# Layer 1's second chunk: transposed and compressed in the last chunk of layer 0 instead of during the first chunk of layer 1

## The chip, the cores and the metric

The kernel runs on one core of a Trainium2 chip. The metric is the device time of one execution in microseconds; the time before is the median of three runs, 926.27 us (924.6 to 926.37). The engines named below are TensorE (PE in the profile; its weight loads are PEld), VectorE (DVE), ScalarE (ACT), GpSimd (POOL) and SyncE (SP), which here only issues transfers.

## The reference, cut to what matters

Two layers work on `x` of 16 sequences, 256 tokens and 256 channels, in float32. Each computes `x = x + s * g` from the layer norm `xn` of `x`. Layer 0 has a diagonal complex recurrence for `s` and a gated two-matrix network with GELU for `g`. Layer 1, cut to its two halves:

```python
kv = x @ Wkv_a
c_kv, k_rope = kv[..., :64], kv[..., 64:]
k_rope = apply_rope(k_rope)
c_kv = c_kv * rsqrt(mean(c_kv * c_kv) + RMS_EPS) * kv_norm_w      # the compressed keys
# q, k_nope and v for 16 heads; k_rope is shared by all heads
attn = softmax(where(mask, q @ k.T * scale, min))                 # causal, within a sequence
s = (attn @ v) @ Wo

probs = softmax(x @ router_w.T + router_b)                        # 8 experts
top_vals, top_idx = top_k(probs, 2)                               # renormalised to sum 1
g = silu(x @ base_w.T + base_b + SCALING * sum_e gate_e * (x @ lora_A[e]) @ lora_B[e])
```

## The kernel before

Tokens are worked on in 8 chunks of 512 (two sequences), `X[ch]` resident in SBUF as four tiles of 128 tokens. All of layer 0 comes first, chunk after chunk, then all of layer 1. The order of every engine is written out by hand: `InOrder` (line 47) chains each instruction of an engine behind the one issued before it, so the program order of the calls is the order on each queue. Since all instructions pass through that helper, the profile gives almost all of them line 53; they are told apart by their tiles.

**Layer 1's stages for a chunk.** `norm_begin` (235) takes the statistics, `norm_end` (248) writes the normalised rows `xn`. `transpose_chunk` (257) turns them with eight TensorE transposes (`tp`), copied to `xnT` by ScalarE. `kv_begin` (266) multiplies `xnT` by `wkva` (16 matmuls into the PSUM tile `pkv`); ScalarE squares the compressed part, VectorE forms the rotated key parts (four products, into thirds of the tile `tmp`) and the mean square `ss`, GpSimd raises it to the power -0.5 (`rk`) and adds the rotated parts into `row`. `kv_end` (293) scales the compressed part into `row`. `key_chunk` (299) turns `row` into `kT`. `router_chunk` (307) makes the router's logits `lg` and the low-rank products `mid`, then on VectorE the gates of the two chosen experts (one Exp on ScalarE among some twenty small instructions), and multiplies `mid` by them. `mid` of one chunk and `tmp` of the next share one buffer.

**Queries** are made per group of four heads, four tiles a group (`query_mm`, 378): tiles 0 and 1 are the rotary halves, multiplied by cosine and sine on VectorE (`query_mul`, 395), combined on GpSimd (`query_rot`, tile `qrot`) and spread into `qg` by eight transfers on SyncE (`query_move`, 419); tiles 2 and 3 are the latent parts, scaled into `qg` by ScalarE (`query_lat`, 405).

**Layer 1's main loop** runs over 64 units, eight to a chunk: unit `i` is one head group for one of the chunk's two sequences. A unit computes scores in three packs (`score_pack`, 1354: matmuls `sc`, VectorE mask and maximum, ScalarE Exp with its sum into `pr`), normalises them on GpSimd (`normalise`, 1386), turns them in 32 x 32 blocks on VectorE (`turn`, 1399, tile `turned`), and stores them to DRAM with four transfers (`send`, 1411, `far`). The next unit but one fetches them back (`fetch`, 1423, `pT`), and `values` (1442) multiplies them by `row`. SyncE's queue in chunk 0 of layer 1 is thus: `qg` of group 0, of group 1, `far` of unit 0, `pT` of unit 0, `qg` of group 2, `far` of unit 1, `pT`, `far` of unit 2, `pT`, `far` of unit 3, `qg` of group 3, and so on. A fetch waits for its store to have landed, and what stands behind it on the queue waits too.

**Where chunk `ch + 1` is prepared.** In the loop: `norm_end(ch + 1)` in unit 2 for later chunks, `transpose_chunk` at the end of unit 2, `kv_begin` at the end of unit 4, `kv_end` in unit 5, `router_chunk` at the end of unit 6, `key_chunk` in unit 7.

**The passage between the layers** is the last chunk of layer 0 (from line 1222). Layer 1's chunk 0 is normalised, turned, compressed and routed there, and the query tiles of group 0 and most of group 1 are made, between the last matmuls of layer 0 (`mix`, tile `pf`; `outs`, tile `py`) and the last additions (`finish0`, 791, tiles `dx` and `x`: two of chunk 7's halves on GpSimd, chunk 6's four instructions on VectorE). Of chunk 1, only `norm_begin(1)` and `norm_end(1)` are there. PSUM tiles of this passage come from a ring of four banks (`ps_mm`, 452), used in turn by every call of `m1` (224); layer 1 then has a pool of five banks for them and one of three for scores (1285), on the same memory. `dtmp`, `stb` and `cst` are tiles of layer 0's pool `w0`, used last by chunk 6's sums (`zf_early`, 967).

Of the kernel before, what the change touches and what calls it, by code (L numbers as in the profile page):

```python
# [11 lines left out]
F32 = mybir.dt.float32  # L12
I32 = mybir.dt.int32
AF = mybir.ActivationFunctionType
ALU = mybir.AluOpType
AX = mybir.AxisListType
PSUM = bass.MemoryType.PSUM

P = 128
# [4 lines left out]
TPC = CH // P  # L24
# [5 lines left out]
NOPE, ROPE, VD, KVL = 128, 64, 128, 64  # L30
# [11 lines left out]
def tile_two_layers(ctx: ExitStack, tc: tile.TileContext, d: dict, out: bass.AP):  # L42
# [162 lines left out]
    def bc_in(ap, n):  # L205

        return ap.unsqueeze(2).to_broadcast([ap.shape[0], ap.shape[1], n])
# [40 lines left out]
    def norm_end(ch):  # L248
        k = chunks[ch]
        k.xn = x1.tile([P, TPC, D], F32, tag="xn", name=f"xn1_{ch}", bufs=1)  # L250
        for j in range(TPC):
            ve.tensor_scalar(
                k.xn[:, j, :], X[ch][:, j, :], k.mv[:, j, 0:1], k.rs[:, j : j + 1],
                ALU.subtract, ALU.mult,
            )
# [7 lines left out]
                pe.transpose(ps[:, j * P : (j + 1) * P], k.xn[:, j, c * P : (c + 1) * P], ident)  # L263
            ac.copy(k.xnT[:, c, :], ps)

    def kv_begin(ch):

        k = chunks[ch]
        k.pkv = pkv = m1(f"pkv_{ch}", [P, TPC, P])
        for j in range(TPC):  # L270
            for c in range(2):
                pe.matmul(
                    pkv[:, j, :], k.xnT[:, c, j * P : (j + 1) * P], wkva[:, c, :],
                    start=(c == 0), stop=(c == 1),
                )
        k.row = ak.tile([P, TPC, P], F32, tag="row", name=f"row_{ch}")
        k.tmp = tmp = ak.tile([P, 3, TPC, KVL], F32, tag="tmp", name=f"tmp_{ch}", bufs=1)
        sq, ra, rb = tmp[:, 0], tmp[:, 1], tmp[:, 2]
        ss = sm1.tile([P, TPC], F32, tag="ss", name=f"ss_{ch}")
        k.rk = sm1.tile([P, TPC], F32, tag="rk", name=f"rk_{ch}")  # L280
        ac.activation(sq, pkv[:, :, 0:KVL], AF.Square)
        x1_ = pkv[:, :, KVL : KVL + HR]
        x2_ = pkv[:, :, KVL + HR : P]
        ve.tensor_tensor(ra[:, :, 0:HR], x1_, rope_k[:, 0], ALU.mult)
        ve.tensor_tensor(ra[:, :, HR:ROPE], x2_, rope_k[:, 0], ALU.mult)
        ve.tensor_tensor(rb[:, :, 0:HR], x2_, rope_k[:, 1], ALU.mult)
        ve.tensor_tensor(rb[:, :, HR:ROPE], x1_, rope_k[:, 2], ALU.mult)
        ve.tensor_reduce(ss, sq, AX.X, ALU.add)
        ve.tensor_scalar(ss, ss, 1.0 / KVL, RMS_EPS, ALU.mult, ALU.add)
        gp.tensor_tensor(k.rk, ss, mhalf, ALU.pow)  # L290
        gp.tensor_tensor(k.row[:, :, KVL:P], ra, rb, ALU.add)

    def kv_end(ch):
        k = chunks[ch]
        sq = k.tmp[:, 0]
        ve.tensor_tensor(sq, k.pkv[:, :, 0:KVL], bc_in(k.rk, KVL), ALU.mult)
        ve.tensor_tensor(k.row[:, :, 0:KVL], sq, bc(kvw_bc, TPC), ALU.mult)

    def key_chunk(ch):
        k = chunks[ch]  # L300
        pk = m1(f"pk_{ch}", [P, CH])
        for j in range(TPC):
            pe.transpose(pk[:, j * P : (j + 1) * P], k.row[:, j, :], ident)
        k.kT = ak.tile([P, CH], F32, tag="kT", name=f"kT_{ch}")
        ac.copy(k.kT, pk)

    def router_chunk(ch):

        k = chunks[ch]
        lg = sm1.tile([P, TPC, NE], F32, tag="lg", name=f"lg_{ch}")  # L310
        mid = ak.tile([P, TPC, P], F32, tag="tmp", name=f"mid_{ch}", bufs=1)
        for jp in range(2):
            pm = m1(f"pm_{ch}_{jp}", [P, 2, 256])
            for j2 in range(2):
                j = 2 * jp + j2
                for c in range(2):
                    pe.matmul(
                        pm[:, j2, 0 : P + NE], k.xnT[:, c, j * P : (j + 1) * P], wmid[:, c, :],
                        start=(c == 0), stop=(c == 1),
                    )  # L320
            ve.tensor_tensor(
                lg[:, 2 * jp : 2 * jp + 2, :], pm[:, :, P : P + NE], bc(rb_bc, 2), ALU.add
            )
            ac.copy(mid[:, 2 * jp : 2 * jp + 2, :], pm[:, :, 0:P])

        def t3(name):
            return sm1.tile([P, TPC, NE], F32, tag=name, name=f"{name}_{ch}")

        def t2(name):
            return sm1.tile([P, TPC], F32, tag=name, name=f"{name}_{ch}")  # L330

        def first_max(l, n, between=None):

            m, fm, eq, oh = t2(f"m{n}"), t2(f"fm{n}"), t3(f"eq{n}"), t3(f"oh{n}")
            ve.tensor_reduce(m, l, AX.X, ALU.max)
            if between:
                between(m)
            ve.tensor_tensor(eq, l, bc_in(m, NE), ALU.is_equal)
            ve.tensor_tensor(eq, eq, desc, ALU.mult)
            ve.tensor_reduce(fm, eq, AX.X, ALU.max)  # L340
            ve.tensor_tensor(oh, desc, bc_in(fm, NE), ALU.is_equal)
            return m, oh

        ex = t3("ex")

        def exps(m):
            ve.tensor_tensor(ex, lg, bc_in(m, NE), ALU.subtract)
            ac.activation(ex, ex, AF.Exp)

        _, oh1 = first_max(lg, 1, exps)  # L350
        l2 = t3("l2")
        ve.scalar_tensor_tensor(l2, oh1, -3e38, lg, ALU.mult, ALU.add)
        _, oh2 = first_max(l2, 2)
        ve.tensor_tensor(oh1, oh1, oh2, ALU.add)
        ve.tensor_tensor(ex, ex, oh1, ALU.mult)
        sw = t2("sw")
        ve.tensor_reduce(sw, ex, AX.X, ALU.add)
        ve.reciprocal(sw, sw)
        ve.tensor_scalar(sw, sw, LORA_SCALE, None, ALU.mult)
        gate = t3("gate")  # L360
        ve.tensor_tensor(gate, ex, bc_in(sw, NE), ALU.mult)
        m3 = mid.rearrange("p j (e r) -> p (j e) r", r=LR)
        ve.tensor_tensor(m3, m3, bc_in(gate.rearrange("p j e -> p (j e)"), LR), ALU.mult)
        k.mg = mid

# [51 lines left out]
    def query_move(n):  # L419
        q = groups[n]  # L420
        for r in range(2):
            for h in range(G):
                sp.dma_start(
                    q.qg[64 + 32 * r : 96 + 32 * r, :, h, :],
                    q.rot[32 * h : 32 * h + 32, r, :].rearrange("p (a q) -> p a q", q=32),
                )


    with ExitStack() as l0:
# [330 lines left out]
        def mix(ch, jp, hT, silu=True, v=nc.vector, a=nc.scalar):  # L760
            pf = mix_mm(ch, jp, hT, pe)
            zf = a2.tile([P, 2, D], F32, tag="zf", name=f"zf_{ch}_{jp}", bufs=3)
            v.tensor_tensor(zf, pf, bc(b2_bc, 2), ALU.add)
            if ch and silu:
                a.activation(zf, zf, AF.Silu)
            return zf
# [9 lines left out]
        def outs(ch, h, dx, v=nc.vector, ring=ps_y):  # L776

            py = [
                ring.tile([P, 2, D], F32, tag="py", name=f"py_{ch}_{b}") for b in range(2)
            ]  # L780
            for j2 in range(2):
                for b in range(2):
                    rows = slice(64 * b, 64 * b + 64)
                    pe.matmul(
                        py[b][:, j2, :], h[rows, j2 * P : (j2 + 1) * P], csc[rows, :],
                        start=True, stop=True,
                    )
            for b in range(2):
                v.tensor_tensor(dx[b], py[b], dx[b], ALU.add)

        def finish0(ch, jp, dx, zf, e=nc.gpsimd):
            js = slice(2 * jp, 2 * jp + 2)
            e.tensor_tensor(dx[jp], dx[jp], zf, ALU.mult)
            e.tensor_tensor(X[ch][:, js, :], X[ch][:, js, :], dx[jp], ALU.add)
# [457 lines left out]
        kv_end(0)  # L1252
        h = recur_out(ch, g, w, v0, g0)
        zf = mix(ch, 0, hT, v=v0, a=a0)
        router_chunk(0)
        key_chunk(0)
        outs(ch, h, dx, v0)
        query_mm(0, 0)
        query_mul(0, 0)
        query_mm(0, 1)  # L1260
        query_mul(0, 1)
        finish0(ch, 0, dx, zf, g0)
        query_rot(0)
        query_move(0)
        for jp in range(2):
            finish0(ch - 1, jp, z6.dx, z6.z[jp], v0)
        zf = mix(ch, 1, hT, v=v0, a=a0)
        ve.tensor_scalar(bb_bc, bb_bc, 0.5, None, ALU.mult)
        query_mm(0, 2)
        query_lat(0, 2)  # L1270
        query_mm(0, 3)
        query_lat(0, 3)
        norm_end(1)
        query_mm(1, 0)
        query_mul(1, 0)
        query_mm(1, 1)
        query_mul(1, 1)
        finish0(ch, 1, dx, zf, g0)
# [324 lines left out]
    for i in range(LAST):  # L1603
# [22 lines left out]
        if r == 2:  # L1626
            gate_end(ch, 1)
            if more and ch:
                norm_end(ch + 1)
        if r == 5 and more:  # L1630
            kv_end(ch + 1)
        if i == LAST - 1:

# [46 lines left out]
            gate_begin(ch, r)  # L1680
        if r == 0 and more and ch:
            norm_begin(ch + 1)
        if r == 2 and more:
            transpose_chunk(ch + 1)
        if r == 4 and more:
            kv_begin(ch + 1)
        if r == 6 and more:
            router_chunk(ch + 1)
# [101 lines left out]
```

## Time and profile before

| | |
|---|---|
| runs | 926.37, 924.6, 926.27 us; median 926.27 us |
| profiled execution | 924.36 us, span on the core 922.6 us |
| TensorE busy | 907.4 us (98% of the span) |
| VectorE, GpSimd, ScalarE busy | 665.9, 570.4, 465.7 us |
| last `pf` matmul of layer 0 ends | 265.2 us |
| first scores of layer 1 (`sc`) start | 273.66 us |
| TensorE idle in 320 to 325 us | 3.4 us of 5 |

Times are microseconds from the start of the span. A line of the timeline gives start, duration, engine, line, operation, the tiles written and read, their shape and a count. A bracket at its end gives the idle time of the engine before it and what released it. A line of windows gives the busy time and instruction count of every engine in that stretch, then the granted TensorE clock as a share of full speed (`PEclk`), the DMA share and GB/s. A line of waits gives who waited for whom, the sum, the number of times and the longest. SPq is SyncE's queue.

### The profile page before, as it was taken

Reading aid. Unit: us, or ns where it says so; the run is one execution under the profiler, and the core shown is the slowest. Engines: PE = TensorE matmul, PEld = TensorE weight load, DVE = VectorE, ACT = ScalarE, POOL = GpSimd, SP = SyncE. Lnnn points to the kernel's source line nnn. Section 1 sums busy time; section 2 is a strip of 40 time slices with the busy share of each in tenths; the row PEclk is TensorE's granted clock in tenths of the full one; section 3 lists DMA queues with packets and bytes.
Section 4 is the critical chain, followed back from the end, with each engine's and each line's share of the span. In section 5 each row is a group of like instructions: output and inputs, shape, how many; then the busy total and the mean of one; then the engine's idle time right before and its main releaser. Section 6 shows DMA issues by size and latency. Waiting matters only on the chain.

```text
span 922.6 us, 17383 instructions
## 1 busy us (share of the span) xinstructions
PE 907.4 (98%) x5426; PEld 696.1 (75%) x5426; DVE 665.9 (72%) x2018; ACT 465.7 (50%) x1529; POOL 570.4 (62%) x885
## 2 busy tenths in 40 slices
PE   8999999999999899999999999999999999999998
PEld 7767888887757566777677777767777776777786
DVE  6875677664687868768967876896787689677662
ACT  3335555654336536545544654554465455446541
POOL 1228687778354527686586768648676864867451
PEclk9999999999999989999999999999999999999999
DMA  9730000000015777677786777777677777767781
GB/s 279 231 115 1 1 2 1 1 1 2 1 26 106 200 195 193 171 199 184 191 200 168 210 179 196 188 190 183 183 207 187 191 187 192 203 161 208 201 234 44
DMA packets 196412, 134.00 MB, mean 145 GB/s; under 512 B 142112, under 2 KB 186976, under 8 KB 196320
## 3 DMA queue, kind: packets, MB, share of 16 engines
q1 hardware_dynamic: 194192, 128.68, 53.2%
q0 software_dynamic: 1152, 3.67, 1.1%
q8 instruction: 44, 0.72, 0.3%
q10 hardware_dynamic: 976, 0.53, 0.2%
q14 instruction: 48, 0.39, 0.1%
HBM read 63.11 MB, written 52.95 MB: 126 GB/s over the span
## 4 chain that ended last, share of the span: by engine, by line
PE 90%; DVE 6%; POOL 1%; DMA 1%; ACT 1%; SPq 1%; issue 0%; DVEq 0%; POOLq 0%; ACTq 0%
PE pq L53 22%; PE sc L53 15%; PE po L53 11%; PE av L53 9%; PE r L53 6%; PE f L53 5%; PE ph L53 5%; PE pf L53 5%; PE pg L53 4%; PE pm L53 2%; PE pkv L53 1%; PE tp L53 1%; DVE w L53 1%; PE pb L53 1%; PE psq L53 1%; DVE st L53 1%
## 5 line engine op out<-in xcount | busy, mean ns | idle before, releaser
L53 ACT ACTIVATE pr<-sc,nm 128x256 f32<-128x256 f32 (+7 forms) x512 | 189.8, 381 | 240.3 <-DVE sr L53 152.3
L53 POOL TENSOR_SCALAR pr<-pr,sr 128x256 f32<-128x256 f32 (+7 forms) x512 | 192.0, 393 | 191.2 <-DVE sr L53 188.8
L53 PEld LDWEIGHTS sc<-kT,qg 128*128 128x128 f32 x1024 | 158.3, 192 | 61.9 <-issue 40.3
L53 PE MATMUL sc<-kT,qg 128*128 128x256 f32 (+7 forms) x1024 | 177.3, 307 | 5.3 <-DMA qg<-qrot 3.4
L53 DVE TENSOR_REDUCE nm<-sc 128x1 f32<-128x256 f32 (+7 forms) x512 | 127.5, 300 | 6.6
L53 DVE STREAM_TRANSPOSE turned<-pr 128x512 f32<-128x512 f32 x186 | 123.1, 687 | 9.2 <-POOL pr L53 9.0
L53 PE MATMUL pq<-xnT,wlat 128*128 128x512 f32 x256 | 124.4, 609 | 0.0
L53 PE MATMUL pq<-xnT,wrope 128*128 128x512 f32 x256 | 120.2, 593 | 0.0
L53 ACT ACTIVATION_READ_ACCUMULATOR pr<-sc,nm 128x1 f32 x512 | 104.3, 204 | 0.0
L53 DVE TENSOR_TENSOR sc<-sc,kmask 128x96 f32<-128x96 f32 (+1 forms) x192 | 45.5, 237 | 66.5 <-PE sc L53 65.5
L53 PE MATMUL av<-pT,row 128*64 128x256 f32 (+1 forms) x1024 | 90.9, 329 | 0.1
L53 POOL TENSOR_TENSOR qrot<-qmul,qmul 128x512 f32<-128x512 f32 x64 | 82.9, 1315 | 8.6 <-DVE qmul L53 3.4
L53 PEld LDWEIGHTS av<-pT,row 128*64 128x64 f32 x1024 | 64.1, 137 | 23.9 <-issue 1.6
L53 DVE TENSOR_TENSOR qmul<-pq,rot_q 128x512 f32<-128x512 f32 x128 | 80.7, 672 | 0.4 <-PE pq L53 0.4
L53 ACT ACTIVATE qg<-pq 64x512 f32<-64x512 f32 x128 | 75.4, 589 | 6.0 <-PE pq L53 5.2
L53 PEld LDWEIGHTS pq<-xnT,wlat 128*128 128x128 f32 x256 | 46.3, 193 | 32.2 <-issue 32.1
L53 PEld LDWEIGHTS pq<-xnT,wrope 128*128 128x128 f32 x256 | 45.7, 191 | 32.4 <-issue 32.1
L53 PEld LDWEIGHTS po<-wout,attT 128*128 128x128 f32 x416 | 58.4, 191 | 9.5 <-issue 4.9
L53 PE MATMUL po<-wout,attT 128*128 128x128 f32 (+1 forms) x416 | 64.5, 308 | 0.0
L53 POOL TENSOR_TENSOR rs<-ve,mhalf 128x4 f32<-128x4 f32 (+1 forms) x17 | 16.8, 986 | 51.9 <-DVE ve L53 36.6
L53 PE MATMUL ph<-xnT,p1T 128*128 128x256 f32 (+1 forms) x128 | 44.3, 503 | 0.8 <-DVE xnT L53 0.8
L53 POOL TENSOR_TENSOR attT<-attT,attT 128x512 f32<-128x512 f32 x36 | 45.1, 1272 | 0.0
(226 smaller groups left out, 1504.3 us busy)
## 6 DMA issues: line engine op xcount, KB each, us to landing
far<-turned SPq DMA_DIRECT2D x248, 192.0 KB, 4.5
pT<-far SPq DMA_DIRECT2D x62, 768.0 KB, 5.0
qg<-qrot SPq DMA_DIRECT2D x256, 64.0 KB, 2.3
x<-in_x_dram SPq DMA_DIRECT2D x7, 512.0 KB, 9.6
out_dram<-x POOLq DMA_DIRECT2D x12, 256.0 KB, 5.1
wqn_wo<-in_wq_nopeT_dram SPq DMA_DIRECT2D x4, 512.0 KB, 4.5
wqn_wo<-in_Wo_dram SPq DMA_DIRECT2D x4, 512.0 KB, 5.7
p2T<-in_proj2T_dram SPq DMA_DIRECT2D x2, 512.0 KB, 7.5
```

The costliest lines, as they stand in the source:

```text
L53: r = getattr(self.engine, name)(*args, **kw)
```

## The change

Chunk 1's `transpose_chunk`, `kv_begin` and `kv_end` move out of units 2, 4 and 5 of chunk 0 into the last chunk of layer 0; later chunks keep their places. There, `norm_end(1)` moves ahead of `outs`. `router_chunk(0)` now returns its second half, the gates, to be run later (`defer`): after `mix(ch, 1)` and after the two copies of `transpose_chunk(1)` on ScalarE's queue. Two query tiles of group 0 stand between the transposes and `kv_begin(1)`, and `kv_end(1)` stands between the two `query_mul` of group 1. `kv_begin(1)` uses three tiles of `w0` in place of `tmp`, since `mid` of chunk 0 is still in that buffer. `query_rot(0)` and `query_move(0)` move ahead of `finish0(ch, 0)`.

```diff
-    def kv_begin(ch):
+    def kv_begin(ch, tmp=None):
...
-        k.tmp = tmp = ak.tile([P, 3, TPC, KVL], F32, tag="tmp", name=f"tmp_{ch}", bufs=1)
-        sq, ra, rb = tmp[:, 0], tmp[:, 1], tmp[:, 2]
+        if tmp is None:
+            t = ak.tile([P, 3, TPC, KVL], F32, tag="tmp", name=f"tmp_{ch}", bufs=1)
+            tmp = [t[:, z] for z in range(3)]
+        k.tmp = tmp
+        sq, ra, rb = tmp
...
-    def router_chunk(ch):
+    def router_chunk(ch, defer=False):
...
+        def gates():
...
+        if defer:
+            return gates
+        gates()
...
-        router_chunk(0)
+        gates = router_chunk(0, defer=True)
         key_chunk(0)
+        norm_end(1)
         outs(ch, h, dx, v0)
         query_mm(0, 0)
         query_mul(0, 0)
         query_mm(0, 1)
         query_mul(0, 1)
-        finish0(ch, 0, dx, zf, g0)
         query_rot(0)
         query_move(0)
+        finish0(ch, 0, dx, zf, g0)
         for jp in range(2):
             finish0(ch - 1, jp, z6.dx, z6.z[jp], v0)
         zf = mix(ch, 1, hT, v=v0, a=a0)
+        transpose_chunk(1)
+        gates()
         ve.tensor_scalar(bb_bc, bb_bc, 0.5, None, ALU.mult)
         query_mm(0, 2)
         query_lat(0, 2)
         query_mm(0, 3)
         query_lat(0, 3)
-        norm_end(1)
+        kv_begin(
+            1,
+            [w0.tile([P, TPC, KVL], F32, tag=n, name=f"kv_{n}") for n in ("dtmp", "stb", "cst")],
+        )
         query_mm(1, 0)
         query_mul(1, 0)
+        kv_end(1)
         query_mm(1, 1)
         query_mul(1, 1)
         finish0(ch, 1, dx, zf, g0)
...
-        if r == 5 and more:
+        if r == 5 and more and ch:
             kv_end(ch + 1)
...
-        if r == 2 and more:
+        if r == 2 and more and ch:
             transpose_chunk(ch + 1)
-        if r == 4 and more:
+        if r == 4 and more and ch:
             kv_begin(ch + 1)
```

More of the change, by code (lines that the diff above doesn't have):

```diff
@@ L294, in kv_end @@
         k = chunks[ch]
-        sq = k.tmp[:, 0]
+        sq = k.tmp[0]
         ve.tensor_tensor(sq, k.pkv[:, :, 0:KVL], bc_in(k.rk, KVL), ALU.mult)
@@ L342, in first_max, with exps @@
             return m, oh
[L344 to L364, printed above, removed]
+        def gates():
+            ex = t3("ex")
+            def exps(m):
+                ve.tensor_tensor(ex, lg, bc_in(m, NE), ALU.subtract)
+                ac.activation(ex, ex, AF.Exp)
+            _, oh1 = first_max(lg, 1, exps)
+            l2 = t3("l2")
+            ve.scalar_tensor_tensor(l2, oh1, -3e38, lg, ALU.mult, ALU.add)
+            _, oh2 = first_max(l2, 2)
+            ve.tensor_tensor(oh1, oh1, oh2, ALU.add)
+            ve.tensor_tensor(ex, ex, oh1, ALU.mult)
+            sw = t2("sw")
+            ve.tensor_reduce(sw, ex, AX.X, ALU.add)
+            ve.reciprocal(sw, sw)
+            ve.tensor_scalar(sw, sw, LORA_SCALE, None, ALU.mult)
+            gate = t3("gate")
+            ve.tensor_tensor(gate, ex, bc_in(sw, NE), ALU.mult)
+            m3 = mid.rearrange("p j (e r) -> p (j e) r", r=LR)
+            ve.tensor_tensor(m3, m3, bc_in(gate.rearrange("p j e -> p (j e)"), LR), ALU.mult)
+            k.mg = mid
+        if defer:
+            return gates
+        gates()
     G = 4
```

## The prediction

> **What bounds the kernel now.** I read the page's busy shares and the chain that ended last, then windows of 5 us around the passage from layer 0 to layer 1, then TensorE's waits there, and last SyncE's timeline, because the one long wait named a transfer.
>
> The page:
>
> ```profile
> PE 907.4 (98%) x5426; PEld 696.1 (75%) x5426; DVE 665.9 (72%) x2018; ACT 465.7 (50%) x1529; POOL 570.4 (62%) x885
> ...
> PE 90%; DVE 6%; POOL 1%; DMA 1%; ACT 1%; SPq 1%; issue 0%; DVEq 0%; POOLq 0%; ACTq 0%
> ```
>
> TensorE is busy nearly throughout, and the change neither adds nor removes a matmul. So only TensorE's idle time can be won or lost, and the time it runs at a lower clock. Both lie together in one place:
>
> ```profile
> core 0: us, PE busy (x) PEld busy (x) DVE busy (x) ACT busy (x) POOL busy (x), PEclk, DMA share, GB/s
> 315.00:320.00 5.00, 5.00 (x26) 3.01 (x22) 4.77 (x13) 2.70 (x11) 2.06 (x5) 1.00 0.96 288
> 320.00:325.00 5.00, 1.60 (x5) 1.00 (x4) 2.21 (x8) 2.06 (x8) 3.20 (x6) 0.81 0.77 102
> 325.00:330.00 5.00, 5.00 (x11) 2.84 (x10) 2.23 (x6) 1.75 (x6) 2.21 (x5) 0.50 0.76 273
> 330.00:335.00 5.00, 5.00 (x52) 4.13 (x51) 2.52 (x10) 2.71 (x10) 0.00 (x0) 1.00 0.79 233
> ```
>
> TensorE stops for 3.4 us and then runs at half clock until about 330. Its waits between 225 and 345 us:
>
> ```profile
> PE sc L53 <- DMA qg<-qrot: 3.4, 1, 3.4
> PE pmT L53 <- ACT qg L53: 0.5, 1, 0.5
> ```
>
> The first is unit 6 of chunk 0 waiting for the rotated queries of head group 3; the second is at the very start of layer 1 (275.1). What makes that transfer late is on SyncE's queue:
>
> ```profile
> 288.21 2.27 SPq L53 DMA_DIRECT2D far<-turned  x4
> 293.20 0.34 SPq L53 DMA_DIRECT2D pT<-far  x1
> 293.70 6.35 SPq L53 DMA_DIRECT2D qg<-qrot  x8
> 300.15 2.48 SPq L53 DMA_DIRECT2D far<-turned  x4
> 305.24 0.34 SPq L53 DMA_DIRECT2D pT<-far  x1
> 305.68 2.33 SPq L53 DMA_DIRECT2D far<-turned  x4
> 312.23 0.34 SPq L53 DMA_DIRECT2D pT<-far  x1
> 312.61 3.20 SPq L53 DMA_DIRECT2D far<-turned  x4
> 315.93 5.87 SPq L53 DMA_DIRECT2D qg<-qrot  x8
> ```
>
> From 288.21 on this queue is never free: it issues, or a `pT` fetch stands at its head until the `far` store before it has landed (gaps of 2.7, 2.6 and 4.2 us). The data were ready earlier: unit 1's last `turned` piece at 296.91 (issued 300.15), unit 2's at 303.75 (305.68), unit 3's at 310.73 (312.61), `qrot` of group 3 at 309.11 (315.93). So from unit 0's `turned` (288.07) to the landing at 323.44 there is one serial chain of 35.4 us on SyncE, in which no compute engine has a part. TensorE needs 320.44 - 288.07 = 32.4 us for its work in that time; the difference is the stall.
>
> **The change, part by part.**
>
> *Transposes and compression ahead of layer 1.* Eight `tp` matmuls and 16 `pkv` matmuls leave units 2 and 4 and go in front of unit 0. The chain prices them, for chunk 0, at 0.88 us (`PE tp`, x8) and 1.98 us (`PE pkv`, x16): together 2.86 us, with no idle TensorE time before 273 to take them. The first scores start 2.86 us later.
>
> *The wait at `pmT`.* It comes from ACT's `qg` of group 1, which shares a PSUM bank with the first `pmT`. With three more tiles in the ring of four, that bank now belongs to `pkv` of chunk 1, freed by the first instruction of `kv_end(1)`. I lay out the new order from rows. VectorE: `xn` right after `lg` at 253.4, four in 1.38 us while GpSimd is idle (the row of `norm_end(0)`), `dx` 1.28, `qmul` as `pq` arrives, last done at 259.6. The four layer-0 additions then run wholly beside GpSimd's `qrot` and its own additions; two of them took 1.64 and 1.75 us beside `qrot` against 0.68 alone, so I take 4 x 1.7, done at 266.4, as late as now. Then `zf` 0.7, on ScalarE Silu 0.63 and the two copies 1.17: `xnT` is whole at 268.9. TensorE reaches `pkv` after `pf` (265.24), `tp` 0.88 and four `pq` (3.44) at 269.6, so 0.7 us of cover; were the copies later, TensorE would stop by the excess. The gates follow: 18 small VectorE instructions of 0.22 us and `mid` 0.69, with Exp behind its table load at 270.4; done at 272.5. ScalarE: `qg` 4 x 0.6 to 272.9, Square 0.4. VectorE: `tmp` 0.88, `ss` 0.6, `qmul` 1.25, then `kv_end` reads `pkv` by 276.5. TensorE wants the bank at 273.84 + 2.86 + 0.8 = 277.5. Cover 1 us. So this wait goes: -0.48.
>
> *Exp's table.* Now ScalarE loads tables three times here (253.84, 255.85, 275.07; 1.28 us each); after, once. Rule against row: the Trainium skill, "ScalarE: Activation LUTs", section "What ACT_TABLE_LOAD costs", has a drain beside the load, some 2.66 us per switch. In this trace the next activation starts 0.01 us after the load (246.17 after 244.88 + 1.28). The two saved are worth 5.3 us by the page and 2.6 by the row, neither on TensorE's path: the first exponentials (276.37) precede the reciprocal at 280.73 with time to spare. I count 0 by either.
>
> *Queries before the additions.* `qrot` of group 0 moves about 2 us earlier on GpSimd, and its eight transfers with it; they are needed at the first score and were in time before. GpSimd then has `rk` 1.0, `row` 0.72 and two additions 2.5 ahead of group 1's `qrot`, so that its eight transfers issue from about 280.5 to 286.3 instead of 274.8 to 280.5. Unit 2 wants them at 294, and the queue is free again before the first `far`. 0.
>
> *Relief inside chunk 0.* VectorE loses `tmp` 0.88, `ss` 0.6 and `kv_end` 0.9 in units 4 and 5, ScalarE 1.17 + 0.4, GpSimd 1.7, TensorE 2.86. All of it lies between 295 and 317, inside the SyncE chain, which waits for none of it. Price: 0. Nothing is added there, so it costs nothing either; the most it could give is the only wait on GpSimd that the trace shows on that queue between 285 and 324, 0.6 us (on `pr`).
>
> *What is late next.* TensorE paces unit 0 (no idle between 275.2 and 320.4), and unit 0's `turned` follows the end of `pg` (281.56) by 6.5 us of unbroken VectorE work. So the chain's start moves with TensorE: 2.86 - 0.48 = 2.38 us. All SyncE items are the same in number and order, so `qg` lands at 325.8. TensorE, freed of 2.86 us, arrives at 320.44 - 0.48 = 319.96 and stands 6.3 us (with the 0.41 from landing to start) instead of 3.4. What was idle before is not filled; the work only went to the side of the chain where nothing hides it.
>
> *The clock after the stop.* In the trace half clock lasts from the restart at 323.85 to about 330.0; half of 6.15 us is 3.1 us lost. The Trainium skill, "TensorE: Matmul & The Clock Gate", section "What's actually happening", says that the clock returns after one busy window of about 3.4 us, and that this window runs free of the kernel. By that the loss would lie between 1.7 and 3.4 us depending on phase. I keep the row, 3.1, hence no difference; with the rule's lower end the sum is 1.4 less. A longer stop can't escape the drop.
>
> **Sum**, against the profiled execution's own 924.36: +2.86 - 0.48 + 0 = +2.38, so 926.74 (925.3 with the short return of the clock). The median of the runs shown, 926.27, is 1.91 above that execution; carried over, 928.65, which I round to **928.6**.
>
> **Rivals.**
>
> *It is nearly even.* The chain shifts as above, but the clock comes back after 3.4 us: 926.27 + 2.38 - 1.4 = 927.2. For it: the three runs differ by 1.8 us, about such a phase. Against: nothing chooses the phase.
>
> *Faster: the change works where the chain of waits points.* That view puts `POOL rk` 0.94, `POOL row` 0.72 and `POOL pr` 0.50 directly before SyncE's transfers of `qg`. If SyncE does wait there, taking `rk` and `row` away would bring the transfers forward. It pays from the point at which the queue regains more than the 2.38 us that its start loses; if it regains the whole 5.9 us that `qg` would be late, the stop (3.41), the `pmT` wait (0.48) and the slow clock (3.1) go: 926.27 - 7.0 = 919.3. Against it: `qrot` was done 6.8 us before its transfer, and SyncE's issues are back to back from 312.23 to 321.8.
>
> *Slower still: the tail itself stops.* If the additions beside GpSimd take 2 us more than I gave them, `xnT` is late by 1.3 us at `pkv`, and `kv_end` holds `pmT` up by about 1: 928.6 + 2.3 = 930.9. For it: the cover is 0.7 and 1 us. Against: both engines' items are counted at their contended price.
>
> **How the numbers follow.** Chances: 0.58 for the sum (its own range 927.5 to 930.0), 0.20 for nearly even, 0.12 for faster, 0.10 for slower still. The range 925.0 to 931.2 reaches over the two neighbours and leaves out the faster case and some of the far slow end. About 0.2%, 1.85 us, is what a measurement of this kernel can tell from no change: slower from 928.1, faster below 924.4. A part of the main case (0.08) falls within that: slower 0.60, same 0.28, faster 0.12.
>
> **What would show it.** The first `sc` near 276.5 instead of 273.66 and no wait at `pmT`; the first `far` issue near 290.6; `qg` of group 3 landing near 325.8; TensorE's wait for it 5 to 6.5 us instead of 3.4; then half clock. I am wrong if that wait shrinks below 3.4 us, if `far` starts no later than 288.2, or if TensorE stops at `pkv` or `pmT`.

## The result, and the profile after

The changed kernel takes 928.18 us (median of 12 runs, 925.95 to 930.09) against 925.15 (12 runs, 922.19 to 927.87) for the kernel before on the same chip: a ratio of 1.0034 with a 95% interval of 1.0024 to 1.0043, so 3.0 us slower (2.2 to 4.0). The forecast was 928.6 and slower, with a sum of +2.38. The profiled execution took 928.56 us (span 926.8) against 924.36 (922.6). Its clock of events is some 0.7 us behind that of the execution before already ahead of the change (`pm` starts at 251.90 against 251.19); this much of any difference in start times below is not the change.

The page of the changed kernel has the same shares as before. Nothing in it points to the change:

```profile
PE 907.9 (98%) x5426; PEld 696.3 (75%) x5426; DVE 664.7 (72%) x2018; ACT 463.4 (50%) x1527; POOL 571.2 (62%) x885
...
PE 85%; DVE 7%; DMA 3%; SPq 2%; POOL 1%; issue 1%; ACT 1%; ACTq 0%; POOLq 0%
```

In the chain of work that ended last (second line) TensorE's share has gone from 90 to 85%, and those of DMA and SyncE's queue from 1% each to 3% and 2%. These shares prove little: the kernel with only the rearrangement, which took no longer (below), shows 86, 2 and 1%. TensorE's timeline from 264 to 282 us shows what was put ahead of the scores (start, duration, idle time before it in brackets):

```profile
265.79 1.04 PE L53 MATMUL tp<-ident,xn 128*128 128x128 f32 x8
266.66 3.60 PE L53 MATMUL pq<-xnT,wlat 128*128 128x512 f32 x8
270.10 1.95 PE L53 MATMUL pkv<-wkva,xnT 128*128 128x128 f32 x16
271.88 3.60 PE L53 MATMUL pq<-xnT,wrope 128*128 128x512 f32 x8
...
277.03 0.97 PE L53 MATMUL sc<-kT,qg 128*128 128x256 f32 x4
278.48 0.66 PE L53 MATMUL pmT<-ident,mid 128*128 128x128 f32 x4 [0.48 <-ACT qg L53]
```

From start to start the transposes cost 0.87 us and the compression 1.78: 2.65 us, with no stop at either. The first scores begin at 277.03 instead of 273.66, 3.37 later, which is 2.65 and the 0.7 that were there before. The last line is a step that I had wrong: the wait of 0.48 us at `pmT` has not gone.

SyncE's queue in the passage that follows:

```profile
291.58 2.27 SPq L53 DMA_DIRECT2D far<-turned  x4
296.57 0.34 SPq L53 DMA_DIRECT2D pT<-far  x1
297.07 6.33 SPq L53 DMA_DIRECT2D qg<-qrot  x8
303.51 2.48 SPq L53 DMA_DIRECT2D far<-turned  x4
308.64 0.34 SPq L53 DMA_DIRECT2D pT<-far  x1
309.08 2.63 SPq L53 DMA_DIRECT2D far<-turned  x4
315.45 0.34 SPq L53 DMA_DIRECT2D pT<-far  x1
315.84 3.38 SPq L53 DMA_DIRECT2D far<-turned  x4
319.33 6.82 SPq L53 DMA_DIRECT2D qg<-qrot  x8
```

This is the list shown of before, item for item, and the offset stays the same to its end: the first `far` is 3.37 later (291.58 against 288.21), the last `qg` 3.40 (319.33 against 315.93). Work that left the middle of the chain has not shortened it anywhere. Only the last item differs, 6.82 us against 5.87. TensorE's waits and its windows around the stop:

```profile
PE sc L53 <- DMA qg<-qrot: 7.0, 1, 7.0
PE pmT L53 <- ACT qg L53: 0.5, 1, 0.5
```

```profile
core 0: us, PE busy (x) PEld busy (x) DVE busy (x) ACT busy (x) POOL busy (x), PEclk, DMA share, GB/s
315.00:320.00 5.00, 5.00 (x32) 3.38 (x29) 4.18 (x11) 3.26 (x16) 2.87 (x8) 1.00 0.62 211
320.00:325.00 5.00, 1.20 (x3) 0.19 (x1) 2.68 (x9) 2.35 (x10) 2.03 (x5) 0.86 0.71 163
325.00:330.00 5.00, 1.80 (x5) 1.58 (x6) 0.00 (x0) 0.00 (x0) 1.82 (x2) 0.50 0.84 154
330.00:335.00 5.00, 5.00 (x17) 2.67 (x17) 2.60 (x8) 2.18 (x6) 1.56 (x4) 0.62 0.65 223
```

TensorE stands 7.0 us instead of 3.4. From 325 to 330 VectorE and ScalarE do nothing at all: like TensorE they wait for what hangs on eight transfers. TensorE restarts at 328.20, against 323.85 before, and the three parts of that difference are all visible: 0.7 of offset, 2.65 of work put ahead, 0.95 for the longer last `qg`. Half clock then lasts to about 333.8 (0.62 is the mean of 3.8 us at 0.50 and 1.2 at 1.00), so some 2.8 us are lost to it, against 3.1 before.

### The profile page after: what moved, and what is told of

It is laid out like the page before. It is cut to its first block, busy times and chain, and to the rows that moved or that the text cites. A ratio compares the mean times of both kernels' runs of the same rounds, so it can differ in the third digit from the quotient of the medians.

```text
span 926.8 us, 17377 instructions
## 1 busy us (share of the span) xinstructions
PE 907.9 (98%) x5426; PEld 696.3 (75%) x5426; DVE 664.7 (72%) x2018; ACT 463.4 (50%) x1527; POOL 571.2 (62%) x885
## 4 chain that ended last, share of the span: by engine, by line
PE 85%; DVE 7%; DMA 3%; SPq 2%; POOL 1%; issue 1%; ACT 1%; ACTq 0%; POOLq 0%
PE pq L53 21%; PE sc L53 14%; PE po L53 9%; PE av L53 9%; PE r L53 6%; PE f L53 5%; PE ph L53 5%; PE pf L53 4%; PE pg L53 4%; SPq L53 2%; PE pm L53 2%; PE pkv L53 2%; DMA far<-turned 1%; PE tp L53 1%; DVE w L53 1%; POOL pr L53 1%
```

## The experiments

The theory from the prediction is that (a) the work put ahead of unit 0 shifts the serial chain on SyncE one for one, (b) the relief behind it is worth nothing because that chain waits for no compute engine, and (c) the stop for `qg`, not TensorE's work, is what the time is made of. The rivals are that the rearrangement itself costs, and that relief gives something back. The first three runs take the change apart, the fourth divides it, the others attack the chain. Medians of the kernel before, on the same chips, were 924.7 to 925.5.

**Only the rearrangement.** The transposes and the compression stay in units 2, 4 and 5; the gates, the additions and the query tiles move as in the change.

```diff
-        transpose_chunk(1)
         gates()
...
-        kv_begin(1, [...])
         query_mm(1, 0)
         query_mul(1, 0)
-        kv_end(1)
...
-        if r == 2 and more and ch:
+        if r == 2 and more:
             transpose_chunk(ch + 1)
```

> The rearrangement of the passage alone (gates later, rows normalised earlier, group 0's transfers earlier), with chunk 1's transposes and key compression left in units 2, 4 and 5. Theory (the loss is the TensorE work put in front of unit 0, which delays the serial SyncE chain): no change, ratio 1.000 to the kernel before, the first far store at 288.2 plus or minus 1 us, TensorE waits 3.4 us for qg of group 3. Rival (the rearrangement itself, or GpSimd's new order, costs): ratio 1.002 to 1.003, and the first far store later by 2 us or more.

924.66 us, ratio 0.9994 (0.9981 to 1.0007). First `far` at 288.26, stop for `qg` of 3.5 us. The rearrangement costs nothing and gives nothing, the two table loads that it saves included.

**Only the added work.** The kernel before, with 8 transposes and 16 matmuls of the same shapes put in the same places, whose results nobody uses; the real ones stay in units 2 and 4.

```diff
+        for c in range(2):
+            ps = m1(f"dt_{c}", [P, CH])
+            for j in range(TPC):
+                pe.transpose(ps[:, j * P : (j + 1) * P],
+                             chunks[0].xnT[:, c, j * P : (j + 1) * P], ident)
         ve.tensor_scalar(bb_bc, bb_bc, 0.5, None, ALU.mult)
...
         query_lat(0, 3)
+        ps = m1("dk", [P, TPC, P])
+        for j in range(TPC):
+            for c in range(2):
+                pe.matmul(ps[:, j, :], chunks[0].xnT[:, c, j * P : (j + 1) * P],
+                          wkva[:, c, :], start=(c == 0), stop=(c == 1))
         norm_end(1)
```

> The kernel before with 8 transposes and 16 matmuls of the same shapes added in front of unit 0, their results unused, and chunk 1's own left where they were: the price without the relief. Theory: first far store 2.65 us later, everything after it too, 927.8 us on a base of 925.2, ratio 1.0029, so within 0.5 us of the changed kernel although TensorE does 2.65 us more work: the relief inside chunk 0 is worth nothing. Rival (the relief is worth its 2.65 us of TensorE time and something else in the change lost it again): 2.65 us slower than the changed kernel, only if that something is present here too; without it, it equals the changed kernel by chance and run e3 shows the gain.

929.46 us, ratio 1.0046 (1.0030 to 1.0061): 4.0 us over its kernel before, where the change costs 3.0. By the medians the relief would be worth 0.9 us, more than the 0.5 us that I had allowed; the two intervals overlap, so it may be nothing. The first `far` is at 292.09, the stop 4.5 us.

**Only the relief.** The kernel before with chunk 1's transposes and key compression left out of units 2, 4 and 5. This kernel leaves work out: chunk 1 reads chunk 0's `xnT` and `row` instead of its own.

```diff
-        if r == 2 and more:
+        if r == 2 and more and ch:
             transpose_chunk(ch + 1)
+        if i == 2:
+            chunks[1].xnT, chunks[1].row = chunks[0].xnT, chunks[0].row
...
-        if r == 4 and more:
+        if r == 4 and more and ch:
             kv_begin(ch + 1)
```

> The relief without the price: the kernel before with chunk 1's transposes, copies and key compression left out altogether (chunk 1 reads chunk 0's xnT and row, so its result is not the reference's). Theory: the SyncE chain from 288.2 to 323.4 stays as it is, TensorE arrives 2.65 us earlier and waits 6.0 instead of 3.4 us, time unchanged within 0.7 us (925.2). Rival (the relief of TensorE, VectorE and GpSimd in units 2 to 5 counts, GpSimd's rk and row releasing SyncE's transfers): at least 2.65 us faster, 922.5 or less, and the transfers of qg start before 315.

924.92 us, ratio 0.9998 (0.9986 to 1.0010): 24 matmuls fewer, and no time gained. TensorE's wait in this run, and the end of SyncE's list:

```profile
PE sc L53 <- DMA qg<-qrot: 7.0, 1, 7.0
```

```profile
288.95 2.27 SPq L53 DMA_DIRECT2D far<-turned  x4
...
317.38 6.19 SPq L53 DMA_DIRECT2D qg<-qrot  x8
```

The stop grew from 3.4 to 7.0 us while the last `qg` is issued as late as ever (28.4 us behind the first `far`; 27.7 before). What TensorE doesn't do, it waits.

**A third of the change.** The changed kernel with the compression back in units 4 and 5; only the eight transposes stay ahead.

```diff
-        kv_begin(1, [...])
...
-        kv_end(1)
...
-        if r == 4 and more and ch:
+        if r == 4 and more:
             kv_begin(ch + 1)
```

> The changed kernel with the key compression of chunk 1 back in units 4 and 5: only its eight transposes stay ahead of unit 0. Nothing is left out. The theory (each us of TensorE work put ahead of unit 0 starts the chain one us later, and the relief behind it is worth nothing): 0.87 of the 2.65 us, so 925.2 + 0.33 x 3.0 = 926.2, ratio 1.001, first scores 0.9 later than before, TensorE's wait for qg about 4.4 us. The rival (the cost lies in the rearrangement around the compression, or in the clock's phase): 925.2 or 928.2, whatever the first scores do.

926.10 us against 925.04, ratio 1.0010 (1.0000 to 1.0019). 0.87 us of work ahead cost 1.1 us (0 to 1.8), 2.65 cost 3.0 (2.2 to 4.0): the medians go with the work, as (a) has it, though this interval alone would also allow no cost. The stop, 5.5 us, was longer than the 4.4 expected; its last `qg` took 7.77 us on the queue.

**The same transfers earlier.** The kernel before; groups 3, 4 and 5 are moved straight behind their `qrot`, in units 3, 5 and 7, ahead of a `pT` fetch.

```diff
             query_rot(n)
+            if i in (3, 5, 7):
+                query_move(n)
...
-            if n is not None and i != 2:
+            if n is not None and i != 2 and i - 1 not in (3, 5, 7):
                 query_move(n)
```

> The kernel before with the transfers of qg put on SyncE's queue straight after their qrot in units 3, 5 and 7 of chunk 0, ahead of the pT fetch and far stores that stood in front. Theory (a serial queue, not the compute engines, makes qg of group 3 late): qg issues from about 308 to 314 and has landed by 317, TensorE does not wait for it at 320.4; a part comes back as a wait for pT of unit 3 in unit 6 (about 1.7 us); 919 to 922 us on a base of 925.2, ratio 0.994 to 0.997. Rival (the transfer engines are full, order does not matter; or GpSimd holds qrot up): the wait for qg stays above 2.5 us and the ratio above 0.999.

A miss: 926.23 us, ratio 1.0009 (0.9998 to 1.0020). The wait for `qg` is gone; TensorE's longest wait and SyncE's list in this run say where it went:

```profile
PE av L53 <- DMA pT<-far: 3.8, 1, 3.8
```

```profile
309.33 7.70 SPq L53 DMA_DIRECT2D qg<-qrot  x8
317.07 0.62 SPq L53 DMA_DIRECT2D pT<-far  x1
317.78 2.20 SPq L53 DMA_DIRECT2D far<-turned  x4
325.44 0.34 SPq L53 DMA_DIRECT2D pT<-far  x1
```

`qg` is out 5 us earlier, but `far` of unit 3, ready at 312.2 in this run, stands behind it until 317.8, and its `pT` until 325.4. The list has no free place: putting one item ahead only chooses which one is late.

**A second queue.** If issuing on SyncE is the limit, a second queue must help. The second four transfers of groups 2 and 3 go to ScalarE's queue, on the kernel before and on the changed one, and to GpSimd's on the changed one.

```diff
-                sp.dma_start(
+                (ac if r and n in (2, 3) else sp).dma_start(
                     q.qg[64 + 32 * r : 96 + 32 * r, :, h, :],
```

> The kernel before, with the second four of the eight transfers of head groups 2 and 3 in chunk 0 issued from ScalarE's queue; nothing is left out. The queue theory (SyncE's serial issuing is the bound in chunk 0): SyncE's queue loses about 3.2 + 2.9 = 6.1 us before group 3 has landed, TensorE's wait of 3.4 us and the half clock behind it (3.1 us) go: 925.2 - 6.5 = 918.7, ratio 0.993. The rival (the transfers themselves are the limit; their 16 engines were 0.96 busy from 315 to 320): the landing stays at about 323 and the time at 925.2, ratio 1.000. A third: ScalarE's four issues, some 3 us each time, stand in order before the exponentials of units 2 and 4, the score banks come free late, and TensorE waits on ScalarE instead: 922 to 925, with that wait in the trace.

> The changed kernel with the same split. Nothing is left out. The queue theory: the whole cost of the change is that its moved work makes SyncE's chain start later; with the chain no longer the bound, TensorE has the same work in both kernels and the change costs nothing: the stop of 7.0 us goes to under 1, ratio to the split kernel before 1.000 within 0.002, so about 918.7, ratio 0.993 to the kernel before. If the transfers themselves are the limit: 928.2, ratio 1.003. If the cost of the change had another source than the chain: 3.0 us over the split kernel before.

> The changed kernel with those eight transfers on GpSimd's queue instead of ScalarE's. Nothing is left out. The queue theory: the relief of SyncE is the same, so the stop goes here too and the time is that of the split over ScalarE within 2 us, 917 to 921; GpSimd has its additions and the scaling of pr in order behind the issues, whose price there no trace of this case shows: if one issue takes 1 us or more, the scaling of pr and with it turned and far are late by 4 us or more, and the gain goes: 922 to 928, with the wait for pr on VectorE in the trace.

On ScalarE's queue: 926.22 us (1.0010, 0.9999 to 1.0022) on the kernel before, 927.55 (1.0029, 1.0017 to 1.0041) on the changed one, so by the medians the change still costs 1.3 us there (the two intervals overlap); on GpSimd's, 925.43 (1.0011, 0.9998 to 1.0024). With ScalarE's queue on the kernel before, SyncE shows:

```profile
294.99 6.97 SPq L53 DMA_DIRECT2D qg<-qrot  x4
302.06 2.49 SPq L53 DMA_DIRECT2D far<-turned  x4
307.14 0.34 SPq L53 DMA_DIRECT2D pT<-far  x1
307.57 4.87 SPq L53 DMA_DIRECT2D far<-turned  x4
...
318.02 5.10 SPq L53 DMA_DIRECT2D qg<-qrot  x4
```

SyncE now takes 6.97 us for four transfers, where it took 6.35 for eight, and 4.87 for a `far` that took 2.33. The last `qg` is out at 323.12; without this run's offset of 1.3 us (first `sc` at 274.98) that is 321.8, just as in the kernel before. So SyncE's own issuing was not the limit, as I had it: its queue and ScalarE's share something that is. TensorE's stop, though, was no longer put down to the transfers:

```profile
PE sc L53 <- DVE qmul L53: 4.2, 1, 4.2
```

VectorE had stood 2.53 us for ScalarE, which had been issuing transfers, so ScalarE's issues did delay TensorE, as the third case had it, though by way of VectorE and without its gain. On the changed kernel the stop for `qg` fell from 7.0 to 4.7 us, not to under 1.

GpSimd's queue relieved SyncE in part. On the changed kernel it shows:

```profile
297.60 2.73 SPq L53 DMA_DIRECT2D qg<-qrot  x4
300.83 4.53 SPq L53 DMA_DIRECT2D far<-turned  x4
```

The four `qg` took no longer than four alone (2.71 us in the run with copies below), though GpSimd issued its own four from 298.70 on; the `far` behind them took 4.53 us instead of 2.48. What SyncE's and ScalarE's queues share is therefore not settled by these runs. The stop on the changed kernel fell from 7.0 to 3.4 us, and the time came to within 0.4 us of the unsplit kernel before; the kernel before with GpSimd's queue was not run, so what the change costs there is open. GpSimd was busy 5.4 us more for the eight.

**Larger pieces.** The kernel before, with `qg` as (head, query, block) and `qrot` as (query, block), so that a transfer writes 2 KB in one piece a partition instead of 16 times 128 bytes.

```diff
-            q.qg = qp.tile([P, CH // 32, G, 32], ...)
+            q.qg = qp.tile([P, G, 32, CH // 32], ...)
...
-                qg[:, b * NQ + a, :, :].rearrange("p h q -> p (h q)"),
+                qg[:, :, :, b * NQ + a].rearrange("p h q -> p (h q)"),
```

> The kernel before, with qg laid out so that each transfer writes 2 KB in one piece on each of its 32 partitions where it wrote 16 pieces of 128 bytes; the bytes, the queue and the order are the same and nothing is left out. Price: the weights of the scores are then read at a stride of 64 bytes, and ScalarE's and GpSimd's writes are at that stride too. If the number of pieces sets the time of a transfer: qg x8 takes under half of its 5.9 to 6.3 us on the queue, the wait for qg goes, 925.2 - 6.5 = 918.7. If the bytes or the issuing set it: qg x8 stays near 6 us, and the time at 925 or above. If strided weight loads are slower than the matmuls they hide behind, the scores cost more and the time rises above 930 in either case; the length of qg x8 on the queue still tells the two apart.

986.35 us, ratio 1.0663 (1.0640 to 1.0686). From 285 to 325 us the packets under 512 bytes fell from 8752 to 528, but the queue hardly noticed:

```profile
297.12 6.05 SPq L53 DMA_DIRECT2D qg<-qrot  x8
```

So the number of pieces does not set the 0.75 us or so of a transfer of 64 KB between 32 partitions and 32 others; what does stays open. The price was elsewhere: the score's weight loads, now at a stride of 64 bytes, took 311 ns instead of 190, and ScalarE's writes 1.04 us instead of 0.59.

**Fewer transfers.** The second four of groups 2 and 3 are not transferred but copied by ScalarE, one copy behind the exponentials of each of the next four score packs, on both kernels.

```diff
+                if r and n in (2, 3):
+                    copies.append((q, h))
+                    continue
                 sp.dma_start(
...
+        q, h = copies.pop(0)
+        ac.copy(
+            q.qg[96:128, :, h, :],
+            q.rot[32 * h : 32 * h + 32, 1, :].rearrange("p (a q) -> p a q", q=32),
+        )
```

> The kernel before, in which half of the eight transfers of head groups 2 and 3 of chunk 0 are replaced by copies on ScalarE, one behind the exponentials of each of the next four score packs; nothing is left out. The split runs showed that a second queue doesn't help: SyncE's four transfers took as long (6.97 us) as its eight had (6.35), so the 16 DMA engines behind the queues seem to be the bound. If they are, taking eight of the sixteen transfers off them (8 x 0.75 = 6 us before group 3 has landed) removes the wait of 3.4 us and the half clock behind it: 925.2 - 6.5 = 918.7, ratio 0.993. If something else sets the landing (the latency from far to pT, a wait on the producers), the wait stays above 2 us and the time at 925. The price on ScalarE, 8 copies of some 0.6 us, is spread over its idle half; if it delays the exponentials enough, TensorE waits for score banks: 921 to 924.

> The changed kernel with the same eight copies. Nothing is left out. If the loss of the change is only that it starts the chain behind the transfers later, it is gone once these transfers are no longer late: the wait for qg (7.0 us) goes to under 1, and the time is that of the copies on the kernel before within 0.2%, about 918.7. If 6 us of relief is not enough, since the wait to remove is 7.0 here and not 3.4: a wait of 0.5 to 1 us with some half clock behind it, 920 to 922. If the loss had another source, 3.0 us over the copies on the kernel before.

925.30 us (1.0004, 0.9993 to 1.0015) and 925.98 (1.0011, 1.0001 to 1.0022). No wait for a transfer is left in either; the changed kernel's waits are now

```profile
PE sc L53 <- ACT qg L53: 4.4, 2, 3.1
PE pmT L53 <- ACT qg L53: 0.5, 1, 0.5
```

The last copy was too far back in ScalarE's order, and TensorE stood for it instead, before units 4 and 6. The times missed the 918.7, and the wait was not gone but had changed its cause. The second expectation, that the change then costs little over the same kernel without it, holds as far as the intervals tell: 0.7 us where it was 3.0.

**The same copies, sooner.** On the kernel before: two at the place of the move, two behind the next pack.

```diff
+                query_copy()    # two copies, behind query_move
...
-        query_copy()            # one, behind each pack
+        query_copy()            # two, behind each pack
```

> The kernel before with the same eight copies as in the run with one copy behind each score pack, but two at the place where the group's transfers are issued and two behind the next pack, so that ScalarE has them done 3 us or more before TensorE wants the group. Nothing is left out. With them in time, far of unit 3 is issued when its data are there (310.7), group 3's four transfers follow at 313.3 and land at about 318.8, before TensorE's 320.4: no stop for qg, no half clock, 925.0 - 6.5 = 918.5, ratio 0.993. Rival: VectorE or ScalarE, up to 1.2 us later through the copies, is next to be late for unit 5 or 6 (a wait on VectorE's qmul of 2 to 4 us stood there with the transfers on ScalarE's queue), and any stop of 2 us or more brings the half clock back: 923 to 925.

924.81 us, ratio 1.0002 (0.9991 to 1.0012). The stop at 320 is gone, as worked out: the last of group 3's transfers is started at 317.0 and TensorE is busy without a break from 300 to 335 at full clock, where the kernel before had lost 6.5 us. But the time is the same. Windows of this run:

```profile
320.00:325.00 5.00, 5.00 (x28) 3.34 (x28) 4.93 (x16) 2.47 (x13) 1.13 (x3) 1.00 0.53 177
325.00:330.00 5.00, 5.00 (x50) 4.42 (x45) 3.73 (x12) 4.72 (x16) 4.25 (x8) 1.00 0.63 158
330.00:335.00 5.00, 5.00 (x22) 3.04 (x21) 4.31 (x25) 2.05 (x10) 2.07 (x5) 1.00 0.89 279
335.00:340.00 5.00, 2.36 (x10) 1.05 (x9) 4.90 (x14) 2.36 (x10) 0.90 (x3) 0.97 0.71 107
340.00:345.00 5.00, 4.18 (x10) 2.93 (x11) 4.90 (x15) 3.53 (x15) 3.30 (x7) 0.50 0.88 280
```

The stop came 17 us later, for VectorE, which is busy 4.90 of 5 us there, and half clock followed it. TensorE's and VectorE's timelines of this run:

```profile
340.82 1.94 PE L53 MATMUL sc<-kT,qg 128*128 128x256 f32 x4 [3.46 <-DVE turned L53]
```

```profile
315.49 0.89 DVE L53 TENSOR_TENSOR tmp<-pkv,rope_k 128x128 f32<-128x128 f32 x4 [3.25 <-ACT tmp L53]
```

VectorE had stood 3.25 us for ScalarE's square of chunk 1's keys (1.30 in the kernel before), behind the copies; how much of the later stop these 2 us make is not separated. So TensorE is held by the transfers at 320 and, in this run in which they are in time, by VectorE at 337, and the stop with its half clock is paid once in either case. In the changed kernel that square is no longer in the passage; these copies on the changed kernel were not tried, and whether they would gain there is open.

## Why the prediction was right

**Right: the work put ahead.** I had 0.88 + 1.98 = 2.86 us; it was 0.87 + 1.78 = 2.65. Nothing hid it, and the chain moved with it, one for one, at two sizes (0.87 and 2.65 us).

**Wrong: "So this wait goes: -0.48".** The step followed the bank of `pmT` through the ring, from the tile of group 1's queries to `pkv`. With the ring shifted by three the wait stayed, at 0.48 us and for the same `qg`. In four runs (before, changed, only rearranged, only work added) `pmT` starts within 0.1 us of the end of the last `qg` that ScalarE reads from layer 0's tiles: 275.07 and 275.11; 278.43 and 278.48; 275.10 and 275.16 (where the trace names VectorE's `sc`, done at about the same time); 278.93 and 278.99. This fits a wait of the new pool's first tile for the last reader of the old pool, whichever bank that had; that reading is argued and not tested. Without the step my sum would have been +2.86, and with the measured work +2.65, so its error and that of `pkv` partly cancelled.

**Too wide: "Both lie together in one place".** The stop is 3.4 of TensorE's 15.2 idle us (922.6 less 907.4); over 7 of the others lie in the first 10 and the last 8 us, where the change reaches nothing.

**Right: the tail holds.** The copies of `xnT` ended at 268.4 with `pkv` at 270.10 (I had 268.9 and 269.6), three of the four additions took 1.64 to 1.75 us beside GpSimd, as priced, and one table load was left. TensorE stopped at neither `tp` nor `pkv`. The slower rival needed a stop there, and had none.

**Right: the relief is worth nothing.** Taken alone, it gave 0.9998 (0.9986 to 1.0010). The faster rival expected SyncE to regain time; its list is as long as before.

**Right in effect, wrong in name: the chain on SyncE.** The list is serial and no compute engine paces it, and the stop grew as I said. But I took SyncE's issuing for the limit, and the split shows that a second queue on ScalarE takes no time out of it. The limit is something that these two queues share; GpSimd's queue, which did relieve SyncE, leaves open what.

**Mis-sized: the stop.** I gave 6.3 us; it was 7.0. It ended later than I had it by 0.95 for the longer last `qg` and 0.27 for the larger shift (2.65 for 2.38), and began later by the 0.48 of `pmT`. I had left the length of that `qg` as it was. It took 5.82 to 6.19 us in three kernels with nothing put ahead (only rearranged, before, only relief), 6.37 to 7.77 in three with work ahead (only work added, changed, transposes only), and 7.70 in the one with earlier moves. With one trace of each, scatter between executions and an effect of the change can't be told apart. The profiled pair differs by 4.2 us, of which 0.7 lay ahead of the change; the medians differ by 3.0.

**The clock.** I kept the measured 3.1 us against the 1.7 of an early return; the loss was 2.8. "Nearly even" needed the early return and did not get it in this execution. That it exists is seen in the changed kernel with GpSimd's queue, where half clock lasted only from 325.2 to 328.6 and 1.7 us were lost (0.66 is the mean of 3.4 us at 0.50 and 1.6 at 1.00):

```profile
325.00:330.00 5.00, 4.92 (x13) 3.19 (x14) 2.23 (x6) 1.52 (x6) 3.50 (x6) 0.66 0.95 297
```

**Luck: the level.** The 928.6 stood on a median of 926.27 for the kernel before, which came out at 925.15 over 12 runs. That base was 1.1 us too high and the change of 2.38 was 0.65 too small, so the agreement to 0.4 us is in part chance. The direction, and the size within the interval of 2.2 to 4.0, are not.

## What to carry to other kernels

Before moving work from a stretch that looks full to one that looks idle, ask which of the two sets the end: here the "full" stretch was already waiting for transfers, so taking work out of it only lengthened the wait, and the same work put ahead of the chain's first link was paid in full. When a stop is removed, find the next engine that has no slack over the following 20 us before counting the gain; here it was VectorE, itself some 2 us later for the copies, and it took the whole 6.5 us back. A second queue is worth trying for a late transfer only with a look at how long the first queue's items take afterwards.

## What the runs showed that I had not expected

- A transfer of 64 KB from 32 partitions to 32 others took 0.67 to 0.97 us on SyncE's queue, averaged over a group of four or eight, with 128-byte or 2 KB pieces alike; with four of ScalarE's issued in between it took 1.74.
- The stretches of half clock came in steps. Summed from the granted clock in windows of 0.5 us, they lasted 6.83 us in the kernel before and in eight other kernels, 10.24 in the changed one, and 3.41 with GpSimd's queue on it and with the copies on it (twice 3.41 with the first copies on the kernel before): one, two or three times 3.41. How much of a stretch falls behind the restart decides the cost, and not the length of the stop alone. In the kernel before the clock fell at 323.1, inside a stop of 3.40 us, and 3.1 us were lost; with GpSimd's queue it fell at 325.2, after a stop of 3.36, and 1.7 were lost; in the changed kernel 2.8 after 7.0. After stops of 2.31 and 1.98 us (first copies) the clock fell too; after one of 1.29 (the same on the changed kernel) it did not.
- A weight load at a stride of 64 bytes took 311 ns against 190, and with 1024 such loads TensorE's busy time rose by 66 us (973.5 against 907.4).
